# A spectral layer cut into 256 blocks at 160 frequencies in place of 128 blocks at 96

## The chip, the cores and the metric

The kernel runs on one core of a Trainium2 chip. The metric is device time in microseconds (us) of one execution, the median over the runs shown. The core has a matrix engine (TensorE, PE in the profile, with its weight loads as PEld), VectorE (DVE), ScalarE (ACT), GpSimd (POOL) and the sync engine (SP). SP and POOL also issue most of the DMAs. TensorE writes to PSUM, from where VectorE and ScalarE take the results.

## What is computed

Two layers on an input of 2 batches, 128 channels and 64x64 positions (L = 4096 tokens). Layer 0: a group norm, a four-head attention with rotary positions, a projection, a residual. Layer 1: a layer norm and a one-head attention over the tokens (`x x^T`, softmax, times `x`), a residual; then a layer norm and a spectral layer, with a residual. The spectral layer, cut to what matters:

```python
U_plus  = causal_conv(phi[:, k], u)             # for each of K = 16 filters, all lags 0..L-1
U_minus = sgn * causal_conv(phi[:, k], sgn * u) # sgn is +1 on even, -1 on odd positions
out  = einsum('btkd,k,kde->bte', U_plus,  sigma**0.25, M_phi_plus)
out += einsum('btkd,k,kde->bte', U_minus, sigma**0.25, M_phi_minus)
out += sum over i < 3 of (u shifted by i) @ M_u[i]
```

Four branches (the first L, L/2, L/4, L/8 tokens) are weighed by a hard choice, of which one remains. `U_plus` and `U_minus` differ in the sign of the odd lags alone, so the kernel holds filters of even and of odd lags (parity s = 0, 1), each mixed by its own matrix: the sum of the two M for even lags, the difference for odd ones.

## The kernel before

**Layer 0** (`layer0`, to 1040 us) goes through four units (batch, pair of heads). The loop over score tiles carries side work: a generator `beside` that is advanced a step at some of the places in a unit. In the last unit that is `beside_last` (L991): the norm of batch 0 for the next attention, the filters' transforms (`filters16`, L876), and the mixing matrices. What is left of it when the loop ends is run after it.

**Attention of layer 1** (`attend16`, L1301), batch 0 from 1040 to 1340 us and batch 1 to 1734 us, carries side work in the same way: for batch 0 `rest16` (L1080: masks, taps); for batch 1 `feed` of batch 0 (L1427) and then, by turns, the first loads of the spectral stage and `feed` of batch 1, what is left of which goes on in the spectral steps.

**How the convolution is cut.** The 4096 tokens are 128 blocks of 32 (NI). Over the blocks, the convolution is done in frequencies (96, NF16); within a block, directly. A step of `feed` takes four token tiles (128 blocks x 128 channels, f32), multiplies them by cosines and by sines (L1482, `pf`), the blocks in two pieces of 64, each on 64 of the array's 128 rows, and writes an upper and a lower f16 half of the result to memory (L1446, L1447, L1487, `rows16`). It also transposes tiles for the taps (`ar`, L1458), and ends with a last shifted transform (`pl`, L1523). The filters are transformed likewise to `tables16`.

**The spectral stage** (`spectral`, L1895) has 48 steps: batch, chunk of 16 frequencies (6), parity of the lags s, parity of the output ro. For each step:

- `fetch` (L1281) loads tokens two steps ahead (POOL, three buffers) and tables (SP, two sets of buffers, one per parity).
- `convolve16` (L1697) makes 8 tiles `pu` of PSUM in bursts of 3, 3 and 2. A tile takes 6 products of 64 rows and 512 columns: three terms (upper x upper, lower x upper, upper x lower) for each of two row groups g, which hold different frequencies. The 64 rows are real and imaginary part x 2 pieces x 16 positions. The 512 columns are 16 output positions x 2 x 16 filters. ScalarE takes the upper half out (L1719), VectorE the lower (L1720), into `xh` and `xl`.
- `mix16` (L1722) mixes the step before: 48 products of 128 x 128 matrices with 512 columns, each as two on 64 rows, which go to two banks of `acc`. It is put between the bursts in three parts. At the end `acc` is added to `oh` (L1738 to L1741).

All products of this stage are kept in the order written (`ordered`), so a burst, a third of the mixing and a step of side work take turns on TensorE. The tag `cv` (three buffers of two banks) holds the bursts' tiles and also those of the side work.

**Back to positions** (`back`, L1799) goes over 4 groups of four positions per (batch, ro): 8 transposes of `oh` (L1857), copies to SBUF (L1858), 8 f32 products with `gw` (L1871), a sum with the attention's part (L1875). Batch 0's runs beside batch 1's steps, (1, 0) beside the last step, (1, 1) after all of them, then the result is written out (L1893).

The loop of the steps:

```python
for _ in convolve16(u, tables_in[s], tokens_in[n % 3], *xs):
    next(late, None)      # a third of the mixing of the step before
    next(beside, None)    # a step of the side work
```

Of the kernel before, what the change touches and what calls it, by code (L numbers as in the profile page):

```python
# [22 lines left out]
P = 128  # L23
# [17 lines left out]
NF = P  # L41
# [6 lines left out]
NF16 = 96  # L48
NCH16 = 6
NS = NF16 // NCH16 // 2  # L50
LAG = 3
# [29 lines left out]
def conv_attn_hybrid(ctx: ExitStack, tc: tile.TileContext, io):  # L81
# [8 lines left out]
    gmat = const.tile([P, P], F32, name="gmat")  # L90
    nc.sync.dma_start(gmat, io["gmat"])
# [13 lines left out]
    nc.gpsimd.memset(spread[NF16:, :NK], 0.0)  # L105
# [31 lines left out]
    def group_norm(b, bank, p1, px):  # L137
# [4 lines left out]
        st = p1.tile([P, NQ, 6], F32, tag="gst", name=f"gst{b}")  # L142
        yield xn
# [30 lines left out]
        xb = xi.rearrange("p (j i) -> p i j", i=NI)  # L174
        for i in range(NQ):
            dst = xn[:, bass.ts(i, 512)].rearrange("p (i j) -> p i j", j=P)
            src = xb[:, 4 * i : 4 * i + 4, :]
            if b == 0 and i >= NQ // 2:
                nc.scalar.activation(dst, src, AF.Identity, bias=bi, scale=sc)
            else:  # L180
                nc.vector.tensor_scalar(dst, src, sc, bi, ALU.mult, ALU.add)
# [17 lines left out]
    def layer0(tok, px, last, side, beside_last):  # L199
# [3 lines left out]
        with ExitStack() as l0:  # L203
# [193 lines left out]
            norm = group_norm(0, bank, p1, px)  # L397
# [33 lines left out]
            for n, (b, pr) in enumerate(units):  # L431
                if n + 1 < len(units):
                    nxt = units[n + 1]
                    if nxt[1] == 0:
                        norm = group_norm(nxt[0], bank, p1, px)
                        xn = next(norm)
                        after = prepare(*nxt, xn)
                        beside = chain(beside, norm, after[3])
                    else:
                        after = prepare(*nxt, xn)  # L440
                        beside = chain(beside, after[3])
# [49 lines left out]
    def layer0_any(tok, px, last, side, beside_last):  # L491

        with ExitStack() as l0:
# [25 lines left out]
            def normed(b):  # L519
                steps = group_norm(b, bank, p1, px)  # L520
# [192 lines left out]
    tables16 = dram.tile([2, 2, NF16 // NS, 2, 2, NDI, NS, 2 * NK], F16, name="tables16")  # L713
    rows16 = [dram.tile([2, 2, DROWS, 2, NF16, C], F16, name=f"rows16_{b}") for b in range(B)]
# [3 lines left out]
    class LayerStats:  # L718


        def __init__(self, p, src, u):
            self.p, self.src, self.u, self.nm = p, src, u, None
            self.mv = p.tile([P, NT, 2], F32, tag="lmv", name=f"lmv{u}", bufs=1)
            self.rs = p.tile([P, NT], F32, tag="lrs", name=f"lrs{u}", bufs=1)

        def take(self, tiles):
            for n, t in enumerate(tiles):
                st = self.p.tile([P, 6], F32, tag="lst", name=f"lst{self.u}_{t}", bufs=2)
# [52 lines left out]
    def layers(st, layer0, in_halves):  # L781
# [70 lines left out]
        def branches16(spare):  # L852

            phi = spare.tile([P, 2, TROW], F32, tag="tab", name="phi16")
            aside.dma_start(phi, io["phi"])
# [9 lines left out]
            turned = new([P, 2, NF16], "turned")  # L865
            aside.dma_start(turned, io["fw16"])
            most = new([P, 8, NK], "phi_most")[:NF16]
# [8 lines left out]
        def filters16(spare):  # L876
            phi, turned, most = chosen[3]
            both = spare.tile([P, 2, L], F16, tag="ks", name="spectra")
            for s, q in ((s, q) for s in range(2) for q in range(2)):
                tb = both[:NF16, q, : 4 * 2 * TROW].rearrange("w (h i x) -> w h i x", h=2, i=2)  # L880
                tbr = tb.rearrange("w h i (o c k) -> w h i c o k", c=2, k=NK)
                lags = slice(0, P // (q + 1))
                for c in range(2):
                    ph = side[0](f"ph{s}_{q}_{c}")[:NF16, :TROW]
                    nc.tensor.matmul(ph, turned[lags, c, :], phi[lags, s, :], start=True, stop=True)
                    nc.vector.tensor_reduce(
                        most[:, 4 * q + 2 * s + c, :], ph.rearrange("w (o k) -> w k o", k=NK), AX.X, ALU.max,
                        apply_absolute_value=True,
                    )
                    ph = ph.rearrange("w (o k) -> w o k", k=NK)  # L890
                    nc.vector.tensor_scalar(tbr[:, 0, 0, c], ph, T_SCALE, None, ALU.mult)
                    nc.vector.scalar_tensor_tensor(
                        tbr[:, 1, 0, c], ph, T_SCALE, tbr[:, 0, 0, c], ALU.mult, ALU.subtract
                    )
                    yield
                    for h in range(2):
                        if c == 0:
                            nc.vector.tensor_copy(tbr[:, h, 1, 1], tbr[:, h, 0, 0])
                        else:
                            nc.vector.tensor_scalar(tbr[:, h, 1, 0], tbr[:, h, 0, 1], -1.0, None, ALU.mult)  # L900
                    yield
                for w in range(NS):
                    part = slice(NF16 // NS * w, NF16 // NS * (w + 1))
                    for h in range(2):
                        aside.dma_start(
                            tables16[s, h, :, :, q, :, w, :].rearrange("b i o x -> b i o x"),
                            tb[part, h].rearrange("b i (o x) -> b i o x", x=2 * NK),
                        )
                yield
            nc.vector.tensor_reduce(spread[:NF16, :NK], most.rearrange("p n k -> p k n"), AX.X, ALU.max)  # L910
# [80 lines left out]
        def beside_last(stage, spare=None):  # L991
            first_parts()
            stages = [stage(n) for n in range(1 if in_halves else 2)]
            stats = LayerStats(last, tok[0], "a0")
# [19 lines left out]
        gw = ffw.tile([P, 2, P], F32, name="gw")  # L1014

        def transform(p):

            fw = p.tile([P, 4, NF16 if in_halves else NF], F32, name="fw", bufs=1)
            aside.dma_start(fw, io["fw_96" if in_halves else "fw"])
# [3 lines left out]
        mask = ffw.tile([P, P], F32, name="mask")  # L1023
        own_mask = ffw.tile([P, 1], F32, name="own_mask")
# [55 lines left out]
        def rest16(p, steps):  # L1080
            wbr, top = chosen[:2]
            ends = p.tile([P, NBR, P], F32, name="ends")
            aside.dma_start(ends, io["ends"].partition_broadcast(P))
            mu_raw = p.tile([P, NBR, NU, C], F32, name="mu_raw")
            aside.dma_start(mu_raw, io["mu"].rearrange("i n d e -> d i n e"))
            ends_T = p.tile([P, NBR], F32, name="ends_T")
            aside.dma_start(ends_T, io["ends_T"])
            aside.dma_start(gw[:NF16], io["gw16"])
            yield from steps
            weighted_sum(mask, ends, top)  # L1090
            weighted_sum(own_mask, ends_T.unsqueeze(2), top)
            yield
            weighted_sum(mu, mu_raw, wbr)
            yield
            own = gw[:NF16]
            nc.vector.scalar_tensor_tensor(
                own, own, OUT_SCALE, mask[:NF16].unsqueeze(1).to_broadcast([NF16, 2, P]), ALU.mult, ALU.mult
            )
# [134 lines left out]
        STEPS = []  # L1233
        for b in range(B):
            for ch in range(NCH16):
                pairs = [(s, ro) for s in range(2) for ro in range(2)]
                if (b, ch) == (B - 1, NCH16 - 1):
                    pairs = [(0, 0), (1, 0), (1, 1), (0, 1)]
                STEPS += [(b, ro, ch, s) for s, ro in pairs]
# [3 lines left out]
        def fetch_tokens(n):  # L1243
            if n >= len(STEPS):
                return
            b, ro, ch, s = STEPS[n]
            row = FIRST[STREAM[ro, s]]
            for half, ut in enumerate(tokens_in[n % 3]):
                for g in range(2):
                    w0 = NS * (2 * ch + g)  # L1250
                    ordered(
                        nc.gpsimd.dma_start(  # L1252
                            ut[64 * g : 64 * g + 64],
                            rows16[b].rearrange("c p r h w d -> (c p) r h w d")[:, row : row + BP, half, w0 : w0 + NS, :],
                        )
                    )
                    yield

        def fetch_tables(ch, s, pieces=1):
            for half, tt in enumerate(tables_in[s]):  # L1260
                own = tables16[s, half, 2 * ch]
                size = BP // pieces
                for part in range(pieces):
                    ordered(
                        nc.sync.dma_start(
                            tt[:, part * size : part * size + size],
                            bass.AP(
                                tensor=own.tensor,
                                offset=own.offset + part * size * NS * 2 * NK,
                                ap=[[NDI * NS * 2 * NK, 8], [NS * 2 * NK, BP], [1, size * NS * 2 * NK]],  # L1270
# [4 lines left out]

        def first_fetch():
            yield from fetch_tables(0, 0, 4)
# [3 lines left out]
        def fetch(n):  # L1281
# [3 lines left out]
            if n == 0:  # L1285
                todo = (0, 1)
            else:
                b, ro, ch, s = STEPS[n - 1]
                rest = [step for step in STEPS[n:] if step[3] == s]
                if not rest or (rest[0][0], rest[0][2]) == (b, ch):  # L1290
                    return
                todo = (rest[0][2], s)
            for _ in fetch_tables(*todo):
                pass
# [132 lines left out]
        def feed(b, p, bank, fw, stats=None, gate=None):  # L1427
# [7 lines left out]
            if in_halves:  # L1435
                to = rows16[b].rearrange("c p r h w d -> w c p (r h) d")
            else:
# [11 lines left out]
            def taps(i, uT):  # L1449
# [12 lines left out]
                queue.dma_start(base[b][:, 4 * i : 4 * i + 4, :], oc)  # L1462
# [3 lines left out]
            for i in range(NQ):  # L1466
                while gate is not None and gate[0] <= i:
                    yield
                un = p.tile([P, 4, C], F32, tag="un", name=f"un{b}_{i}")
                if in_halves:  # L1470
                    stats.prepare(range(4 * i, 4 * i + 4), own_mask)
# [3 lines left out]
                for c in range(2):  # L1475
                    at = BP + 1 + 2 * i
# [640 lines left out]
```

## Time and profile before

| what | value |
|---|---|
| median of 3 runs | 2601.43 us (2595.63 to 2602.68) |
| profiled execution, its own time | 2609.66 us |
| its span, first to last instruction | 2607.8 us |
| granted TensorE clock, mean | 0.984 |
| busy: TensorE / weight loads | 2464.1 us (94%) / 1203.5 us (46%) |
| busy: VectorE / ScalarE / GpSimd | 1545.1 us / 1769.4 us / 488.6 us |
| moved by DMA | 227.10 MB |

How to read it: a line of a group gives the source line, the engine, the operation, what it writes and reads by the program's names, the shape, the count, then busy time and mean duration of one, then the idle time of the engine just before such instructions with what ended it. A TensorE form `64*128 64x512` is 64 rows of contraction, 128 columns of weights, 512 columns moved. Busy time is a union, so overlapping products count once. An f32 product leaves two records. A timeline line begins with the start and the length in us; a line of a windows table has the stretch, its length, then busy time and instruction count of each engine, granted clock, DMA share and GB/s.

### The profile page before, as it was taken

Reading aid. Unit: us, or ns where it says so; the run is one execution under the profiler, and the core shown is the slowest. Engines: PE = TensorE matmul, PEld = TensorE weight load, DVE = VectorE, ACT = ScalarE, POOL = GpSimd, SP = SyncE. Lnnn points to the kernel's source line nnn. Section 1 sums busy time; section 2 is a strip of 40 time slices with the busy share of each in tenths; the row PEclk is TensorE's granted clock in tenths of the full one; section 3 lists DMA queues with packets and bytes.
Section 4 is the critical chain, followed back from the end, with each engine's and each line's share of the span. In section 5 each row is a group of like instructions: output and inputs, shape, how many; then the busy total and the mean of one; then the engine's idle time right before and its main releaser. Section 6 shows DMA issues by size and latency. Waiting matters only on the chain.

```text
span 2607.8 us, 37833 instructions
## 1 busy us (share of the span) xinstructions
PE 2464.1 (94%) x14787; PEld 1203.5 (46%) x14787; DVE 1545.1 (59%) x2854; ACT 1769.4 (68%) x2055; POOL 488.6 (19%) x773
## 2 busy tenths in 40 slices
PE   5999999999999999999989989879999999999996
PEld 3555555555544445444433334334444444444444
DVE  6256366236617542978786565676666665666653
ACT  4999999999999988666665555545445444455541
POOL 2022022002304432100033321132211111111100
PEclk9999999999999999999998989999999999999999
DMA  5122122002205533767566667644444443544421
GB/s 153 37 63 60 54 69 53 7 15 75 63 5 80 101 57 28 139 120 133 101 113 127 120 114 136 103 96 111 107 104 106 105 101 84 136 104 98 98 49 59
DMA packets 329469, 227.10 MB, mean 87 GB/s; under 512 B 286816, under 2 KB 289536, under 8 KB 323392
## 3 DMA queue, kind: packets, MB, share of 16 engines
q1 hardware_dynamic: 277008, 141.92, 26.4%
q0 software_dynamic: 50832, 80.24, 14.9%
q8 instruction: 118, 1.93, 0.3%
q10 hardware_dynamic: 1440, 2.43, 0.3%
q14 instruction: 71, 0.58, 0.1%
HBM read 117.84 MB, written 26.64 MB: 55 GB/s over the span
## 4 chain that ended last, share of the span: by engine, by line
PE 39%; DVE 8%; DMA 7%; issue 3%; ACT 2%; SPq 1%; POOL 0%; DVEq 0%; ACTq 0%; POOLq 0%
PE m L1730 18%; PE cv L1708 9%; DMA eT<-pair 5%; PE od L1340 3%; DVE pair L1326 2%; PE y L1312 2%; PE oa L1340 2%; DVE both L1360 2%; PE bk L1871 1%; DMA tables_b<-tables 1%; PE pf L1482 1%; PE ar L1458 1%; ACT ey L1321 1%; PE vt L1857 1%; SPq L1331 1%
## 5 line engine op out<-in xcount | busy, mean ns | idle before, releaser
L470 ACT ACTIVATE e<-s 128x1536 f16<-128x1536 f32 (+1 forms) x704 | 938.0, 1426 | 49.1 <-PE s L214 44.5
L1719 ACT CAST x<-cv 128x1024 f16<-128x1024 f32 x384 | 365.9, 1018 | 307.0 <-PE cv L1708 304.7
L1720 DVE TENSOR_TENSOR x<-cv,x 128x1024 f16<-128x1024 f32 x384 | 448.2, 1219 | 202.1 <-ACT x L1719 201.9
L214 PE MATMUL s<-qs,ks 128*128 128x512 f16 x2048 | 560.3, 381 | 7.9 <-ACT e L470 3.8
L214 PE MATMUL acc<-e,v 128*97 128x512 f16 x2048 | 559.5, 380 | 8.4 <-DVE accs L418 5.9
L1730 PE MATMUL m<-x,mxr 64*128 64x512 f16 x3072 | 466.7, 376 | 0.0
L214 PEld LDWEIGHTS <-v 128*97 128x97 bf16 x2048 | 255.3, 125 | 222.7 <-issue 22.1
L1321 ACT ACTIVATE ey<-y,nshift 128x512 f32<-128x512 f32 x288 | 196.1, 686 | 194.3 <-PE y L1312 151.1
L214 PEld LDWEIGHTS <-ks 128*128 128x128 f16 x2048 | 200.8, 99 | 233.5 <-issue 51.0
L1730 PE MATMUL m<-x,mxl 64*128 64x512 f16 x1536 | 293.3, 377 | 0.0
L1730 PEld LDWEIGHTS <-mxr 64*128 64x128 f16 x3072 | 152.0, 94 | 179.9 <-issue 1.0
L1360 DVE SCALAR_TENSOR_TENSOR both<-eT 128x512 f16<-128x512 f16 x224 | 153.6, 686 | 115.6 <-DMA eT<-pair 113.2
L1312 PE MATMUL y<-bothT 128*128 128x512 f16 x864 | 206.2, 382 | 3.9 <-ACT ey L1321 3.0
L1252 POOL DMA_DIRECT2D tokens<-rows x192 | 117.6, 618 | 441.4 <-PE cv L1708 404.6
L1340 PE MATMUL od<-pair,hi 128*128 128x512 f16 x576 | 190.4, 392 | 9.9 <-DVE oT L1352 9.0
L1326 DVE TENSOR_TENSOR pair<-ey,pair 128x1024 f16<-128x1024 f32 x144 | 174.8, 1217 | 26.6 <-ACT pair L1325 26.3
L1708 PEld LDWEIGHTS <-tokens 64*128 64x128 f16 x2304 | 112.2, 94 | 154.1 <-issue 27.9
L418 DVE COPY accs<-acc 97x512 f32<-97x512 f32 x64 | 44.2, 691 | 213.6 <-PE acc L214 213.6
L1340 PEld LDWEIGHTS <-hi 128*128 128x128 f16 x1024 | 102.0, 100 | 134.2 <-issue 21.7
L1325 ACT CAST pair<-ey 128x1024 f16<-128x1024 f32 x144 | 150.6, 1046 | 5.9 <-DMA eT<-pair 3.6
L1708 PE MATMUL cv<-tables_b,tokens 64*128 64x512 f16 x1152 | 138.3, 379 | 8.3 <-DMA tables_b<-tables 5.7
L1340 PE MATMUL oa<-eT,hi 128*128 128x512 f16 x448 | 145.3, 385 | 0.0
(222 smaller groups left out, 2414.0 us busy)
## 6 DMA issues: line engine op xcount, KB each, us to landing
tokens<-rows POOLq DMA_DIRECT2D x192, 128.0 KB, 9.7
tables_b<-tables SPq DMA_DIRECT2D x24, 1024.0 KB
tables_e<-tables SPq DMA_DIRECT2D x22, 1024.0 KB
tab<-in_rot SPq DMA_DIRECT2D x32, 512.0 KB
rows<-uh POOLq DMA_DIRECT2D x128, 96.0 KB, 3.2
ks<-term POOLq DMA_DIRECT2D x112, 64.0 KB, 2.2
qs<-term POOLq DMA_DIRECT2D x112, 64.0 KB, 2.0
accs<-back SPq DMA_DIRECT2D x32, 128.0 KB
```

The costliest lines, as they stand in the source:

```text
L214: tc.keep_in_program_order(nc.tensor.matmul(*args, **kw))
L470: nc.scalar.activation(e[:, own, :], ps[:, own, :], AF.Exp, scale=SCORE_SCALE)
L1312: nc.tensor.matmul(ps[:, q, :], a[0][:, bass.ts(t, P)], c[0][:, bass.ts(i, 512)], start=(n == 0), stop=(n == 2),)
L1321: nc.scalar.activation(e[:, q, :], ps[:, q, :], AF.Exp, bias=nshift16, accum_out=den[:, t, i : i + 1])
L1325: nc.scalar.copy(pair[:, 0, own], e)
L1326: nc.vector.tensor_tensor(pair[:, 1, own], e, pair[:, 0, own], ALU.subtract)
L1340: nc.tensor.matmul(acc, a[0][:, own], pair(m, t), start=(start and t == 0 and n == 0), stop=(stop and t == 3 and n == 2),)
L1360: nc.vector.scalar_tensor_tensor(both, eT[:, 0, :, u, :], 1.0, eT[:, 1, :, u, :], ALU.mult, ALU.add, accum_out=den[:, 4 * i + u, j : j + 1],)
L1708: nc.tensor.matmul(pu[:, g, :], ut[own, at, :], tt[own, :, at, :], start=(n == 0), stop=(n == 2))
L1719: nc.scalar.copy(hi, pur)
L1720: nc.vector.tensor_tensor(lo, pur, hi, ALU.subtract)
L1730: nc.tensor.matmul(acc[:, g, :], m[lines], x[lines], start=(i == 0), stop=(i == len(products) - 1))
```

## The change

Blocks of 16 tokens, 256 of them (two halves of 128, NB), 160 frequencies (NF16), pieces of 64 blocks as before but four of them. The 64 rows of a convolution product are now 2 x 4 pieces x 8 positions, and its 512 columns are 2 lag parities x 8 output positions x 2 x 16 filters, so that one product serves both parities. There are 40 steps: batch, chunk of 16 frequencies (10), half of a chunk. A step has 8 tiles, one per (input parity `par`, frequency of the half). Each tile is taken out in two pieces per engine, by lag parity, to the output parity `par ^ s`. The mixing has 96 products (parity s now inside) of 256 columns: 2 output parities x 4 frequencies x 2 groups x 16.

```diff
-NF16 = 96
-NCH16 = 6
+NB = 2
+BQ = NI // 4
+NF16 = 160
+NCH16 = 10
 NS = NF16 // NCH16 // 2
+HS = NS // 2
+PARTS = (107, 107, 106)
+BACKS = (0, 53, 106)
+NBACK = 54
...
+        STEPS = [(b, ch, half) for b in range(B) for ch in range(NCH16) for half in range(2)]
...
+        def fetch_tables(n):
...
+            row = NS * 2 * NK
+            for half, tt in enumerate(tables_in[n % 2]):
+                for s in range(2):
+                    for g in range(2):
...
+                            nc.sync.dma_start(
+                                tt[64 * g : 64 * g + 64, BQ * s : BQ * s + BQ + s],
...
+        def convolve16(u, half, tables, ut, xs):
+            th, tl = tables
+            items = [(par, at) for par in range(2) for at in range(HS)]
             for burst in BURSTS:
                 pus = []
+                for par, at in (items[n] for n in burst):
+                    pu = pc.tile([P, 2, 512], F32, tag="cv", name=f"cv{u}_{par}_{at}", bufs=3)
+                    for n, (h, tt) in enumerate(((0, th), (1, th), (0, tl))):
...
+                                    ut[own, par, at, h, :],
+                                    filters_of(tt, own, par, HS * half + at),
...
                 yield
+                for par, at, pu in pus:
+                    pur = pu.rearrange("d g (s o k) -> d s k g o", s=2, k=NK)
+                    for s in range(2):
+                        hi, lo = (
+                            x[:, s].rearrange("d k (r w g o) -> d r w k g o", r=2, w=HS, g=2)[:, par ^ s, at] for x in xs
+                        )
+                        nc.scalar.copy(hi, pur[:, s])
+                        nc.vector.tensor_tensor(lo, pur[:, s], hi, ALU.subtract)
+                yield
+        def mix16(ch, half, xh, xl, acc, ohs):
+            products = [(m[:, k, s, :], xh[:, s, k, :]) for s in range(2) for k in range(NK) for m in (mxl, mxr)]
+            products += [(mxr[:, k, s, :], xl[:, s, k, :]) for s in range(2) for k in range(NK)]
...
+                if (i + 1) % (2 * NK) == 0:
                     yield
+            for ro, oh in enumerate(ohs):
+                part = acc[:, :, P * ro : P * ro + P].rearrange("e n (w q c) -> e n w q c", w=NS, c=2)
...
+                nc.scalar.copy(own, part[:, 0])
+                nc.vector.tensor_tensor(own, part[:, 1], own, ALU.add)
```

In the loop of the steps the evictions of a burst now come ahead of the side work. The other parts of the diff:

- `filters16`: eight groups (four shifts of 64 blocks, lines 128 and 32 of the frequencies) in place of four, each for cosine and sine; products over 256 lags are two accumulated ones where both halves hold something. The table's last dimension stays 32 f16 values (64 bytes) to a write.
- `feed`: three transforms (107, 107 and 106 lines of cosines and sines together) for four token tiles in place of two; the shifted last transform `pl` falls away; a half's edge is carried to the other half.
- `back16` in place of `back`: 4 groups of two positions per (batch, ro), with transposes of 108 columns for each of three parts (`BACKS`) and f32 products of 256 columns. For batch 1 the first two parts run beside the steps from the eighth chunk on, the third after the last step.

```diff
+            for q2 in range(BQ // 2):
...
+                for q, pt in enumerate(pair):
+                    for n, m in enumerate(chunks):
+                        ordered(nc.tensor.transpose(pt[:, n, :], ohr[:, BQ - 1 - 2 * q2 - q, own], ident))
+                for q, pt in enumerate(pair):
+                    (nc.scalar.copy if q else nc.vector.tensor_copy)(v[:, q, own, :], pt[:, own, :])
+                yield
+                for q in range(2):
+                    for n, m in enumerate(chunks):
...
+                                pt[:, q, :], v[:, q, n, :], gw[:, m, :], start=(n == 0), stop=(n == len(chunks) - 1)
...
+                nc.vector.tensor_tensor(dst, pt, hads[q2] if begin else dst, ALU.add)
```

- `gw` is scaled and masked at the start of batch 1's steps (`inverse_of`) in place of `rest16`; masks have 256 columns; the matrix `gmat` of the group norm is loaded anew for each batch; one buffer in place of two for the mixing matrices' loads; the statistics of the last unit move to other buffers; the tokens of a group norm are put in the order of the new halves.

## The prediction

> **What bounds the kernel now.** I read the stages first, then the groups of one stage, then the order of TensorE's work. By windows cut at the stage borders (0 to 1040 layer 0, to 1340 and to 1734 the attention of batch 0 and 1, to 2574 the spectral steps, then the tail):
>
> ```profile
> core 0: us, PE busy (x) PEld busy (x) DVE busy (x) ACT busy (x) POOL busy (x), PEclk, DMA share, GB/s
> 800.00:1040.00 240.00, 229.56 (x1029) 115.54 (x1027) 123.20 (x305) 221.26 (x169) 89.17 (x112) 0.99 0.47 67
> 1340.00:1734.00 394.00, 351.79 (x1428) 150.16 (x1426) 248.16 (x580) 219.45 (x460) 102.25 (x144) 0.94 0.64 117
> 1900.00:2142.00 242.00, 242.00 (x2243) 109.05 (x2240) 162.39 (x149) 123.05 (x133) 38.77 (x64) 1.00 0.47 102
> 2574.00:2608.00 34.00, 16.26 (x134) 14.79 (x132) 9.84 (x13) 2.91 (x5) 0.00 (x0) 0.89 0.17 65
> ```
>
> From 1900 to 2142 nothing but spectral steps runs: TensorE is busy all 242 us and issues 2243 products, 107.9 ns each. A step has 48 products of the convolution and 96 of the mixing, so it takes 144 x 107.9 = 15.54 us, and 48 steps take 746 us. VectorE has 162 of 242 us, ScalarE 123. So the spectral stage is bound by TensorE, and the question is what a step costs there. Groups of 1900 to 2100 by form:
>
> ```profile
> L1730 PE MATMUL m<-x,mxr 64*128 64x512 f16 x830 | 125.6, 376 | 0.0
> L1720 DVE TENSOR_TENSOR x<-cv,x 128x1024 f16<-128x1024 f32 x104 | 121.3, 1219 | 53.8 <-ACT x L1719 53.8
> L1719 ACT CAST x<-cv 128x1024 f16<-128x1024 f32 x104 | 99.0, 1018 | 86.5 <-PE cv L1708 86.1
> ```
>
> The mixing never waits (0.0); VectorE and ScalarE wait for TensorE, not it for them. TensorE's order of time, three answers:
>
> ```profile
> 1951.85 0.38 PE L1730 MATMUL m<-x,mxl 64*128 64x512 f16 x2
> 1952.06 0.38 PE L1730 MATMUL m<-x,mxr 64*128 64x512 f16 x2
> ...
> 1851.34 0.60 PE L1523 MATMUL pl<-un,fw 64*96 64x128 f32 x8
> ...
> 2592.52 3.74 PE L1871 MATMUL bk<-gw,whole 96*128 96x128 f32 x32
> ```
>
> Two products on 64 rows each run as a pair, one pair per 215.5 ns, though one record lasts 376 ns.
>
> **Main step: 48 steps become 40, and the mixing's products become half as wide.** The convolution keeps 48 products of 512 columns a step: 48 x 107.9 ns = 5.18 us. The mixing goes from 96 products of 512 columns to 192 of 256: the same columns, twice the products and weight loads. The trace has no f16 product of 256 columns, so this is bounded from both sides. Below: half of 215.5, 108 ns a pair. Above: nothing hidden, the width's 108 plus one 94 ns weight load (mean of the mixing's loads), 202. Two rows lie near. An f32 record takes twice as long per column: six `ar` records of 512 columns take 2.74 us, one alone 0.592, so (2.74 - 0.592) / 5 = 430 ns. An f32 record of 128 columns thus streams as long as an f16 one of 256. The `bk` row (one row group): (3.74 - 0.275) / 31 = 112 ns per load and product. The `pl` row has the very form of the new mixing, pairs on 64 rows, each with its own loads: 8 in 0.60 us, one alone 0.269, so (0.60 - 0.269) / 3 = 110 ns a pair, with f32 loads that last longer (159 ns) than the f16 ones (94).
>
> A rule of the Trainium skill speaks against it: "TensorE: Matmul & The Clock Gate", section Back-to-back issue gap, has streams of weight load and product at some 81 ns a product for 128 columns, whatever the formula for an isolated one gives. If a load and its product cost 81 ns here too, a pair takes 162. The `pl` row says 55 a product, but for 8 products that could have been queued; 192 in a row are not shown. I take 110 and keep 162 as a rival.
>
> Step after: 5.18 + 96 x 0.110 = 15.74 us; 40 steps 630 us. **746 - 630 = 116 us gained.** Each ns of the pair costs 96 x 40 = 3.84 us.
>
> **The engines beside it.** The 8 evictions of 1024 elements by each engine become 16 of 512. Rows of this size: ScalarE 586 ns (`oh<-m`), VectorE 690 (`oh<-m,oh`). ScalarE: 16 x 0.586 + 2 x 0.27 for the accumulator = 9.9 us of 15.74; VectorE 16 x 0.69 + 2 x 0.3 = 11.6. Both stay below TensorE. Within a burst, six VectorE pieces end about 5.6 us after its start, and the third buffer is wanted at 6.7. So these cost nothing while TensorE is the slower; uncovered, VectorE sets the step (a rival). The writes are runs of 32 bytes; L891 writes such runs (96x496) in 653 ns, no slower. Token loads stay four of 128 KB a step. Tables become 2.2 MB each two steps after 2.1 MB, again asked for two steps ahead: hidden. The one stall for them (5.7 us, the first `tables_b`) I keep.
>
> **Feed (to frequencies).** Two transforms for every four token tiles become three, so the 128 `pf` records become 192. Four records (one transform) take 0.86 us (1.02 less the 0.16 that one record's end takes). In the spectral steps the last three sets of token tiles stay over as before: 3 more transforms, +3 us, less the `pl` work and stall (1.5), plus about 2 of waits for the shared buffers: +3. In the attention of batch 1: 13 more, 11 us; the waits there grow by half, less the `pl` stall:
>
> ```profile
> PE pf L1482 <- DVE uh L1447: 12.4, 10, 2.9
> PE pl L1523 <- DVE oc L1461: 5.6, 1, 5.6
> PE uT L1504 <- DVE uh L1447: 5.0, 3, 3.3
> ```
>
> (17.4 + 4.8 for `un`) / 2 = 11, less 6 for `pl` and less some 4 as gaps overlap: with the products **+12 us**. POOL issues 192 row writes for 128 at 0.68 us, behind token loads on the same queue; it has 102 of 394 us busy, so this is hidden.
>
> **Filters in layer 0.** In 800 to 1040 TensorE is busy 230 and ScalarE 221 of 240 us: no room on either. The filters' f32 products go from 8 (two records each, 0.83 us) to 24 of 0.86: +14 us TensorE. VectorE gets 96 operations for 40, +25 us; it has 117 us idle there, but each holds the one bank that the output projection uses: +3. The side work needs 100 turns where the loop offers 96, and now used 80: the last four run after it, with 3 us of VectorE exposed at most. 64-byte table writes grow from 47,616 to 81,920 and are needed only some 500 us later. **+17 us.** Masks twice as wide in attention 0: +1.
>
> **Back.** Before, a group of four positions takes 8 transposes (1.1 us) and 16 records of `bk` (1.95), and waits 0.78 us between the transposes: 3.8 us, 10 groups before the last mixing ends, 38 us. After, a group of two takes 6 transposes (0.85) and 12 records of 256 columns (0.216 each, 2.6): 8 groups for batch 0, 28 us; for batch 1 two thirds beside the steps, 18 us; some 2 us of waits, the transposes now standing before both copies. 48 less 38: **+10**. Tail: before 24.8 us from the last mixing product to the last sum. After, 8 groups with a third each; every one waits in a ring, copy 0.27, products 1.02, sum 0.95 (L1875 takes 1.03), signals 0.2: 2.45 us, with the accumulator's eviction 21.5. **-3.** The output's 9.6 us stay.
>
> **Sum.** -116 + 3 + 12 + 17 + 1 + 10 - 3 = -76; first ramp of the steps (VectorE's 16 x 0.69 after 8 x 1.22) +1: -75. The profiled execution took 2609.7 us (span 2607.8), so 2534.7; the median of the runs stands 8.2 below it: 2601.4 - 75 = **2526 us**.
>
> **Rivals.**
> - *Loads or issue set the mixing's pace* (other side). For: four instructions per 110 ns is twice the present rate, and 480 a step for 288; the rule above. Against: `pl` at that very rate. At 162 ns, + 52 x 3.84 = 200: 2726. It decides from 110 + 75 / 3.84 = 129.5 ns on; at 135 the time is 2622. Chance 0.16.
> - *VectorE becomes the bound.* For: strided sums (L1875) take 1.03 us at 512 elements where others take 0.69. At that price 16 x 1.03 + 0.8 = 17.3 us a step, less what of the back and feed work on TensorE now lies beneath it: about +35, 2561. Against: the 32-byte runs of L891. Chance 0.12.
> - *Side work costs double* (filters and feed, 29 us more, by in-order waits in both): 2555. For: TensorE's 42 idle us in attention 1 lie around such waits. Chance 0.12.
> - *Side work is absorbed* in the idle 10 us of layer 0's end and 42 of attention 1: 2500. Chance 0.10.
>
> **How the numbers follow.** The forecast's chance is 0.50; its own range is 2505 to 2550 (pair 108 to 114, side terms by half). A difference under 0.3% (7.8 us) can't be told from none. Faster: 0.50 + 0.10 + 0.12 + 0.09 of VectorE's = 0.81; same 0.03, from VectorE's far end; slower 0.16. The range reaches from the absorbed case to where pairs stand near 135 ns: 2490 to 2622; past it remain 0.12 above and 0.05 below.
>
> **What would show it.** Right: in mid-stage, pairs of `m` start every 110 ns, TensorE busy throughout, steps of 15.7 us, the spectral stage some 105 us shorter, layer 0 some 17 and attention 1 some 12 longer. Wrong: pairs further apart with no releaser named (issue); `cv` waiting for DVE `x`; `po` or `pf` waiting for VectorE by tens of us.

## The result, and the profile after

The changed kernel takes 3088.45 us (3081.52 to 3095.21), 1.187 times the time before (95% interval 1.183 to 1.191). The forecast was 2526 us, with a range of 2490 to 2622. The profiled execution has a span of 3093.4 us and a mean granted clock of 0.899 (0.984 before).

Cut at the same events as before (first score of each batch's attention, first product of the convolution, last of the mixing), in us, with the experiment that matters most beside it (e1: the same change with pieces of 112, 112 and 96 lines):

| stage | before | after | after - before | e1 | e1 - before |
|---|---|---|---|---|---|
| layer 0 | 1041.1 | 1065.6 | +24 | 1064.3 | +23 |
| attention, batch 0 | 276.2 | 304.0 | +28 | 303.4 | +27 |
| attention, batch 1 | 417.1 | 896.4 | +479 | 452.7 | +36 |
| spectral, to the last mixing | 839.1 | 792.8 | -46 | 747.8 | -91 |
| tail | 34.3 | 34.7 | 0 | 35.3 | +1 |

The loss lies in one stage, the attention of batch 1. The windows of that stage and of the middle of the spectral stage, of the changed kernel (columns as before: the stretch, its length, busy time and count by engine, clock, DMA share, GB/s):

```profile
1370.00:2266.00 896.00, 442.92 (x1568) 180.32 (x1567) 300.42 (x681) 248.28 (x515) 450.51 (x193) 0.73 0.72 64
2800.00:3055.00 255.00, 254.21 (x3692) 188.68 (x3688) 168.98 (x278) 137.37 (x268) 35.20 (x53) 1.00 0.33 86
```

In the spectral steps TensorE works 254 of 255 us. In the attention of batch 1 it works 443 of 896; POOL is busy 451 us there, where it had 102 of 394. The waits of 1370 to 2266 us (who waits, for whom, sum, times, longest):

```profile
ACT uh L1461 <- DMA rows<-uh: 345.7, 21, 30.8
...
DVE uh L1462 <- ACT uh L1461: 275.4, 21, 33.0
...
PE uT L1530 <- DVE uh L1462: 211.8, 12, 28.6
...
PE pf L1504 <- DVE uh L1462: 129.1, 17, 21.4
```

Read from the top, this is a chain. ScalarE may write `uh`, of which there are two buffers, only when the row writes out of it have landed. VectorE stands behind ScalarE, and TensorE behind VectorE for the next transform or transpose; what the attention has behind these in the engines' order waits with them. ScalarE's group of these evictions over the whole kernel, before and after:

```profile
L1446 ACT ACTIVATE uh<-pf 96x512 f16<-96x512 f32 x64 | 37.1, 592 | 56.4 <-PE pf L1482 50.2 <-DVE uh L1447 5.2 <-DMA rows<-uh 0.6
...
L1461 ACT ACTIVATE uh<-pf 107x512 f16<-107x512 f32 (+1 forms) x96 | 55.6, 596 | 501.3 <-DMA rows<-uh 388.0
```

The wait for the row writes was 0.6 us and is 388, in 24 pieces, each of which ends 0.1 to 0.4 us after the last row write of the transform two before has landed. The row writes themselves, as groups of POOL and as DMA issues with the median from issue to landing, before:

```profile
L1487 POOL DMA_DIRECT2D rows<-uh x128 | 87.1, 686 | 120.9 <-DVE uh L1447 98.8 <-DMA tokens<-rows 12.4 <-DVE both L1360 4.4
...
rows<-uh POOLq DMA_DIRECT2D x128, 96.0 KB, 3.2
```

and after:

```profile
L1509 POOL DMA_DIRECT2D rows<-uh x192 | 517.8, 2700 | 232.5 <-DVE uh L1462 138.5 <-issue 91.4 <-DMA rows<-uh 1.4
...
rows<-uh POOLq DMA_DIRECT2D x128, 107.0 KB, 15.0
...
rows<-uh POOLq DMA_DIRECT2D x64, 106.0 KB, 20.2
```

A write of 107 or 106 KB in place of 96 KB costs POOL four times as long to issue (2700 ns mean for 686) and lands some five to six times as late (15.0 and 20.2 us for 3.2). The forecast had 192 of them at 0.68 us.

What the forecast was about did happen. TensorE's order of time in the spectral steps of the changed kernel (start, length, products of the run):

```profile
2884.59 2.11 PE L1751 MATMUL cv<-tables_b,tokens 64*128 64x512 f16 x18
2886.54 0.27 PE L1779 MATMUL m<-x,mxl 64*128 64x256 f16 x2
2886.65 0.27 PE L1779 MATMUL m<-x,mxr 64*128 64x256 f16 x2
...
2889.92 0.27 PE L1779 MATMUL m<-x,mxr 64*128 64x256 f16 x2
2890.03 2.11 PE L1751 MATMUL cv<-tables_b,tokens 64*128 64x512 f16 x18
```

From 2886.54 to 2889.92 are 31 pairs, 109.0 ns each, and a burst with its third of the mixing takes 5.44 us (2890.03 - 2884.59), as 18 x 107.9 ns + 32 x 110 ns = 5.46 us would have it.

### The profile page after: what moved, and what is told of

The parts are those of the page before. It is cut to its first block, busy times and chain, and to the rows that moved or that the text cites. A ratio compares the mean times of both kernels' runs of the same rounds, so it can differ in the third digit from the quotient of the medians.

```text
span 3093.4 us, 44325 instructions
## 1 busy us (share of the span) xinstructions
PE 2458.0 (79%) x17459; PEld 1364.1 (44%) x17459; DVE 1543.5 (50%) x3219; ACT 1777.5 (57%) x2399; POOL 926.4 (30%) x800
## 3 DMA queue, kind: packets, MB, share of 16 engines
q0 software_dynamic: 134560, 90.46, 19.0%
q10 hardware_dynamic: 1440, 2.43, 0.2%
## 5 line engine op out<-in xcount | busy, mean ns | idle before, releaser
L1509 POOL DMA_DIRECT2D rows<-uh x192 | 517.8, 2700 | 232.5 <-DVE uh L1462 138.5
L1767 ACT CAST x<-cv 128x512 f16<-128x512 f32 x640 | 355.2, 589 | 271.4 <-DVE x L1768 172.7
L1768 DVE TENSOR_TENSOR x<-cv,x 128x512 f16<-128x512 f32 x640 | 415.7, 686 | 174.3 <-ACT x L1767 169.7
L1779 PE MATMUL m<-x,mxr 64*128 64x256 f16 x5120 | 433.4, 270 | 0.0
L1461 ACT ACTIVATE uh<-pf 107x512 f16<-107x512 f32 (+1 forms) x96 | 55.6, 596 | 501.3 <-DMA rows<-uh 388.0
L1779 PE MATMUL m<-x,mxl 64*128 64x256 f16 x2560 | 287.2, 271 | 1.3 <-DVE oh L1789 1.3
L1779 PEld LDWEIGHTS <-mxr 64*128 64x128 f16 x5120 | 253.5, 95 | 46.5 <-issue 1.2
L1462 DVE SCALAR_TENSOR_TENSOR uh<-pf,uh 107x512 f16<-107x512 f32 (+1 forms) x96 | 64.2, 685 | 327.5 <-ACT uh L1461 327.4
L1504 PE MATMUL pf<-un,fw 64*107 64x512 f32 (+1 forms) x192 | 86.3, 739 | 150.7 <-DVE uh L1462 130.4
L1530 PE MATMUL uT<-ident,un 128*128 128x128 f32 x64 | 16.4, 406 | 218.0 <-DVE uh L1462 218.0
```

Source lines behind the costliest of these rows:

```text
L1509: queue.dma_start(rows16[b][r, 2 * part + q, at : at + 2, lines].rearrange("t w h d -> w t (h d)"), uh[:, q, 2 * r : 2 * r + 2].rearrange( ...
L1767: nc.scalar.copy(hi, pur[:, s])
L1768: nc.vector.tensor_tensor(lo, pur[:, s], hi, ALU.subtract)
L1779: nc.tensor.matmul(acc[:, g, :], m[lines], x[lines], start=(i == 0), stop=(i == len(products) - 1))
```

## The experiments

Three questions: what makes the row writes slow, what took the main step's gain once they are mended, and whether a version exists that keeps it.

My theory after the result: the count of lines of a row write is what hurts, 107 being prime and 106 = 2 x 53. The Trainium skill, "DMA: Bandwidth & Descriptors", section "Why a DMA increments its semaphore by 16 and not by 1", says that a transfer runs on as many of the 16 engines as the largest number up to 16 that divides the slowest dimension of both its sides: 16 for 96 lines, 1 for 107, 2 for 106. It names an exception for POOL's queue that could have spared these writes, so the rule is put to the test. Rivals: more writes on POOL's queue, or a busier memory, whatever the count.

**e1 and e2: the same change with other pieces.** The three transforms have 320 lines together however they are cut.

```diff
-PARTS = (107, 107, 106)
+PARTS = (112, 112, 96)      # e2: (128, 128, 64)
```

> The changed kernel, the three transforms of feed cut into 112, 112 and 96 lines in place of 107, 107 and 106; nothing else. Uneven-lines theory (a row write whose line count has no divisor near 16 is issued slowly and lands late): POOL's row writes fall from 2.7 us each to about 0.7 and land in 3 to 5 us instead of 15, the attention of batch 1 goes from about 890 back to some 405 us, the kernel to 2540 to 2580 us. Rival, count theory (half again as many writes and transforms through two buffers): nothing of this, the kernel stays above 2950 us.

> The changed kernel with parts of 128, 128 and 64 lines. Uneven-lines theory: within 15 us of the run with 112, 112 and 96. If the number of lines in one write counts, and not its divisors, it is slower than that run by more than 15 us. Count theory: above 2950 us.

Measured: e1 2608.78 us, ratio 1.0025 (1.0014 to 1.0035); e2 2605.9 us, 1.002 (1.001 to 1.0029). The number of writes is the same 192. The row writes of e1:

```profile
L1509 POOL DMA_DIRECT2D rows<-uh x192 | 125.2, 658 | 161.4 <-DVE uh L1462 156.9
...
rows<-uh POOLq DMA_DIRECT2D x128, 112.0 KB, 2.5
...
rows<-uh POOLq DMA_DIRECT2D x64, 96.0 KB, 2.9
```

One constant takes away 480 us: larger writes (112 KB) land after 2.5 us, and the mean issue takes 658 ns. The number of writes and their bytes are not the cause. ScalarE's wait for the writes falls from 388 to 21.1 us. Still, e1 only comes level with the kernel before; 2540 to 2580 us were expected, and the attention of batch 1 at 405 us, where it takes 452.7. The later experiments look for this rest.

**e3 and e4: the kernel before, each row write split in two.** In e3 at an odd place, in e4 in halves.

```diff
-queue.dma_start(to[:, c, q, 2 * own : 2 * own + 4, :], uh[:, q, 2 * r : 2 * r + 2]...)
+for w in (slice(0, 53), slice(53, NF16)):      # e4: (slice(0, 48), slice(48, NF16))
+    queue.dma_start(to[w, c, q, 2 * own : 2 * own + 4, :], uh[w, q, 2 * r : 2 * r + 2]...)
```

> The kernel before, each row write of 96 lines issued as two, of 53 and 43 lines; nothing else of the change. Uneven-lines theory: 256 writes at about 2.5 to 3 us each on POOL and landing late: slower by 250 to 600 us, all of it in the attention of batch 1 and the first spectral steps. Count theory: the same time as the run with two of 48 lines.

> The kernel before, each row write of 96 lines issued as two of 48. Uneven-lines theory: 256 writes at about 0.65 us each: at most 25 us slower. Count theory: slower by 100 us or more, as the one with 53 and 43.

Measured: e3 3349.24 us, ratio 1.287 (1.284 to 1.290); e4 2604.24 us, 1.0015 (1.0001 to 1.0029). In e3:

```profile
L1488 POOL DMA_DIRECT2D rows<-uh x256 | 523.1, 2046 | 540.0 <-issue 488.3
...
L1446 ACT ACTIVATE uh<-pf 96x512 f16<-96x512 f32 x64 | 36.5, 591 | 483.0 <-DMA rows<-uh 335.7
...
rows<-uh POOLq DMA_DIRECT2D x128, 53.0 KB, 20.6
rows<-uh POOLq DMA_DIRECT2D x128, 43.0 KB, 19.1
```

and in e4:

```profile
L1488 POOL DMA_DIRECT2D rows<-uh x256 | 148.0, 586 | 108.0 <-DVE uh L1447 72.2
...
rows<-uh POOLq DMA_DIRECT2D x256, 48.0 KB, 2.3
```

The fault can be put into the kernel before, by nothing but the place of a cut: the same bytes in the same 256 writes differ by 745 us (3349.24 - 2604.24). That is the theory's sharpest test (e3 was expected 250 to 600 us slower; it is 748). The writes of 43 lines land after 19 us with less than half the bytes of the 96 KB write that lands in 3.2.

**e5: 108, 108 and 104 lines.** None of these is a multiple of 16; the largest divisors up to 16 are 12, 12 and 13.

> The changed kernel with parts of 108, 108 and 104 lines. If a write goes over as many DMA engines as the largest number up to 16 that divides its lines (12 and 13 here), it is nearly as quick as with 112, 112 and 96: at most 40 us slower than that run. If only multiples of 16 are quick and every other count takes the slow way of 107, it stays above 2950 us.

Measured: 2614.02 us, ratio 1.0059 (1.0041 to 1.0077). POOL takes 758 ns a write, landing 2.7 us (108 lines) and 4.2 (104). So it needs no 16: 12 or 13 come within 0.3 to 0.4% of it. Only counts whose largest divisor up to 16 is 1 or 2 were slow here; what lies between was not run.

**e10: the 107-line writes issued by SP.** Is it POOL's issue that costs, or the transfer?

```diff
-                                queue.dma_start(
+                                nc.sync.dma_start(
```

> The changed kernel with its 107, 107 and 106 lines, the row writes issued by the sync engine's hardware queue in place of POOL's. Issue theory (POOL makes the descriptors of an uneven write one by one, 3.1 us each, and that alone is the loss): the writes land in 3 us or so, the kernel at 2590 to 2660 us. Spread theory (an uneven write goes over one or two DMA engines whoever issues it): they land in 7 us and more, ScalarE waits for its two buffers, and the transposes of the attention stand behind the writes on the same queue: 2700 to 3100 us.

Measured: 3146.1 us, ratio 1.210 (1.208 to 1.212). ScalarE's group of the row evictions, with what ended its idle time:

```profile
L1461 ACT ACTIVATE uh<-pf 107x512 f16<-107x512 f32 (+1 forms) x96 | 55.9, 597 | 513.2 <-DMA rows<-uh 377.9 <-PE pf L1504 127.0 <-DVE uh L1462 6.8
```

With POOL out of it ScalarE waits 378 us for the same writes (388 in the changed kernel). So the loss goes with the writes and not with POOL. SP is slow to issue them too (4.9 us median, 0.2 at the least), and the attention's transposes stand in the same queue, so this run alone does not part issue from transfer. In the changed kernel the two can be told apart: a 107-line write takes 3.1 us to issue and lands 15 us after its issue began, so most of the time lies behind the issue.

The sizes of the packets in the traces show how the writes were spread. On SP's queue in e10 the rows are 40,960 packets of 512 bytes, just their data, and 256 packets of 4 bytes come with them: one for each of the 128 writes of 107 lines, two for each of the 64 of 106. On POOL's queue the changed kernel has, against e1, more packets of 24 bytes (1920 = 128 x 15), of 8 bytes (896 = 64 x 14) and of 32 bytes (61,568 = 128 x 15 x 26 + 64 x 14 x 13). That fits one reading: a 107-line write sends its data over one DMA engine, as 26 packets of 4096 bytes and one of 3072, and a 106-line write over two, as 13 of 4096 and one of 1024 on each; every engine without data gets as many small packets. These counts of engines, 1 and 2, are those of the rule tested here, on both queues. e10 has no small packets and loses as much, so they are not needed for the loss.

**e6: a seventh turn of side work in the last part of layer 0** (on e1). e1 leaves some 50 us over the kernel before in layer 0 and the attention of batch 0. TensorE stands there right after the first scores of batch 0, in e1:

```profile
PE y L1329 <- ACT ey L1338: 23.2, 2, 21.3
```

ScalarE has not yet taken these scores out. The profile names the loads of the masks as what ScalarE waits for, but the landings tell otherwise: the last table write of the filters is issued after layer 0's loop and lands at 1087.8 us, ScalarE starts at 1088.4, and the masks' loads land after that (`ends` 1091.6, `ends_T` 1094.3). So it is the last table writes that hold it. Before, the last of them had landed at 1006.8 us, 34 us ahead of the first scores.

```diff
-BESIDE_LAST = (0, 1, 3, 5, 6, 9)
+BESIDE_LAST = (0, 1, 3, 5, 6, 9, 10)
```

> Parts of 112, 112 and 96, and the side work of layer 0's last unit is also advanced at the tenth score tile (7 turns a row of tiles in place of 6, 112 in all for the 100 needed). Late-writes theory (the last filter group is emitted after the loop, its eight table writes hold the start of attention 0 by some 21 us): the first wait of TensorE in attention 0 for ScalarE is gone, the kernel 15 to 27 us faster than with 112 lines alone, about 2585. Rival, loads theory (that wait is for the masks' and taps' loads, which come after layer 0 in any case): within 6 us of that run.

Measured: 2606.87 us, ratio 1.002 (1.0008 to 1.0031), no gain where 15 to 27 us were expected. The 21-us wait is gone (3.0 us in three), the attention of batch 0 is 22 us shorter (280.9), and layer 0 is 25 us longer (1089.0). TensorE's output projection `po` now waits for VectorE's `ao`:

```profile
PE po L224 <- DVE ao L392: 20.8, 2, 11.4
```

The stall moved.

**e7 and e8: the scaling of the inverse table `turn`** (on e1). At about 1991 us, POOL issues the load of `turn`; VectorE stands at its scaling until it has landed, and TensorE waits for the convolution's evictions behind it. Waits of e1 from 1960 to 2030 us (the load is named here by another DMA of the same queue):

```profile
DVE turn L1967 <- DMA had<-base: 13.9, 1, 13.9
...
PE cv L1751 <- DVE x L1768: 12.4, 2, 12.0
```

e7 makes the scaling a step of the side work, three turns after the load; e8 keeps it in that place in VectorE's order as well:

```diff
-            nc.vector.scalar_tensor_tensor(turn, turn, OUT_SCALE, own, ALU.mult, ALU.mult)
-            return turn
+            def scaled():
+                ordered(nc.vector.scalar_tensor_tensor(turn, turn, OUT_SCALE, own, ALU.mult, ALU.mult))  # e7: without ordered
+                yield
+            return turn, scaled()
...
-                    beside = chain([None] * 3, *parts, guard(one_bank))
+                    beside = chain([None] * 3, scaled, *parts, guard(one_bank))
```

> Parts of 112, 112 and 96, and the inverse transform's matrices are scaled three turns after their load is issued, not right behind it. Blocked-queue theory (VectorE stands 13.9 us before the scaling, and the convolution's evictions stand behind it): TensorE's one wait of 12.0 us for VectorE at the start of batch 1's steps is gone, 8 to 13 us faster than with 112 lines alone. Rival: the wait comes from draining the side work at that place, and stays: no difference.

> The kernel with pieces of 112, 112 and 96 lines, and with the scaling of the inverse transform's table kept at its place in VectorE's order, three turns of the side work after its load is issued (moving the line in the program alone changed nothing: VectorE still stood 11.9 us for the load). Theory that VectorE's 13.9-us stand at the table's load is what costs TensorE the 12.0-us wait for the convolution's eviction at the change of batch: 2597 to 2600 us, 9 to 12 us under the 2608.8 of the same kernel without it, and the long wait of cv for x gone. Rival, that the stand is only moved to the first product of the way back, or was covered by other work: 2606 to 2611 us.

Measured: e7 2607.52 us, ratio 1.0023 (1.0003 to 1.0042), with VectorE still standing 11.9 us at 2005 us: its place in the program did not move it, and it stays some 200 us ahead of the first product that reads `turn` (2211 us in e1). e8 2592.46 us, ratio 0.9966 (0.9954 to 0.9977), somewhat more than the 9 to 12 us expected: the long waits of `turn` and of `cv` are gone, and the spectral stage is 15 us shorter than in e1 (732.8).

**e13: table writes in runs of 128 bytes** (on e1). The table writes of the filters land after 9.8 us in e1, 5.5 before; layer 0's last round trips through memory (4 KB each) and the first loads of the attention run among them. The two halves of a number are put side by side in memory, and a buffer holds four frequencies with both halves in place of eight with one. Bytes and products stay.

```diff
-    tables16 = dram.tile([2 * NCH16, 2, 2, 2, 4, NDQ, NS, 2 * NK], F16, name="tables16")
+    tables16 = dram.tile([2, 2 * NCH16, 2, 2, 4, NDQ, HS, 2, 2 * NK], F16, name="tables16")
...
-                            tables16[first : first + groups, :, :, :, q, :, w, :].rearrange(
-                                "b s h i o x -> b (s h i) o x"
+                            tables16[w // HS, first : first + groups, :, :, q, :, w % HS].rearrange(
+                                "b s i o h x -> b (s i) o (h x)"
```

> The kernel with pieces of 112, 112 and 96 lines, and with the filters' tables laid out in DRAM so that each piece of a table write is 128 bytes for 64 (the two halves of a number side by side): 40,960 pieces for 81,920, where the kernel before has 47,616; products, evictions and fetched bytes as they are. Theory that the pieces of the table writes hold up layer 0's small round trips and the start of attention 0: landing of the table writes back from 9.8 us to about 5, the 21-us wait at attention 0's start mostly gone, layer 0 and attention 0 together 25 to 40 us shorter than the 50 us that they have over the kernel before, so 2570 to 2585 us. Rival, that layer 0 is longer for the filters' products and evictions themselves (14 us of TensorE more): not more than 8 us gained, 2600 to 2610 us.

Measured: 2581.94 us, ratio 0.9912 (0.9898 to 0.9926). The table writes of e1:

```profile
tables<-spectra POOLq DMA_DIRECT2D x32, 128.0 KB, 9.8
```

and of e13:

```profile
tables<-spectra POOLq DMA_DIRECT2D x32, 128.0 KB, 6.2
```

TensorE's wait at the start of the attention, in e13:

```profile
PE y L1329 <- ACT ey L1338: 13.8, 2, 11.9
```

Layer 0 and the attention of batch 0 are 22 us shorter than in e1 (1345.4 for 1367.7 together), a little less than the 25 to 40 expected: the wait went from 21.3 to 11.9 us, not to nothing. The last table write lands at 1065.1 us and ScalarE starts at 1065.7, 15 us after the first scores (24 in e1); VectorE's operations on the filters last as long as they did or 0.1 us less. So the small runs account for 22 of the 50 us that these two stages had lost.

**e14 and e15: both together, and with the seventh turn.**

> Both of the last two edits on the pieces of 112, 112 and 96 lines: 128-byte pieces in the table writes, and the scaling of the inverse table at its place. If both losses are what the theory says, they add, for they lie in different stages: 2558 to 2575 us, faster than the kernel before. If each is covered by a wait behind it: 2600 to 2608 us.

> The last kernel with a seventh turn of the side work in each step of layer 0's last part, so that the filters end before attention 0 begins. With the long pieces of 64 bytes this moved the stall from attention 0 to layer 0 and gained nothing. If the stall is the writes' traffic, then with half of the pieces there is nothing left to move: within 6 us of the kernel without the seventh turn. If it is the filters' work on TensorE and VectorE, a seventh turn gains up to 15 us in attention 0 and loses up to 25 in layer 0.

Measured: e14 2570.92 us, ratio 0.9876 (0.9861 to 0.9891); e15 2568.19 us, 0.9875 (0.9859 to 0.9891). The two edits nearly add, as edits in different stages should (27 us for e13 and 16 for e8 against e1's median, 38 together), and e14 is 1.2% faster than the kernel before. In e15 the attention of batch 0 is 15 us shorter than in e14 and layer 0 12 us longer, with no net gain. With the writes eased, this is the pattern that e15's expectation gave to the filters' own work: it has to be done in one of the two stages. That is read from the stages; no run took this work away alone, and the time by itself (within 6 us of e14) fits both theories of that expectation.

## Why the prediction was wrong

**The step that failed** is in the part on the feed: "POOL issues 192 row writes for 128 at 0.68 us ... so this is hidden". The duration came from a row for 96 lines, and was carried to 107 lines as if only the count of writes mattered. It measured 2.70 us to issue and 15 to 20 us to land, and the second is what costs: `uh` has two buffers, so the whole feed goes at the writes' pace. e1 undoes just this and is 480 us shorter by the medians, 490 by the profiled spans. Of the 490, 444 lie in the attention of batch 1 and 45 in the spectral steps (896.4 - 452.7, 792.8 - 747.8), where the rest of the feed runs. None of my rivals was this one. The pieces (107, 107 and 106) stood in the change, and what such counts do to a DMA could have been looked up; I weighed a rule on TensorE's issue and not the one on DMAs.

Mended, e14's stages can be held against the sum:

| term | forecast | measured (e14 - before) |
|---|---|---|
| spectral stage: main step, feed there, back, ramp | -102 | -105 |
| feed in the attention of batch 1 | +12 | +37 |
| filters in layer 0, masks | +18 | +9 in layer 0, +18 in the attention of batch 0 |
| tail | -3 | +3 |
| sum | -75 | -37 (span 2570.6 for 2607.8) |

**Main step: right.** 110 ns a pair were forecast from eight `pl` products; 109.0 were measured over 31 pairs in a row, in step after step. The rival of loads and issue (162 ns) fell, and so did VectorE as the bound: TensorE works 254 of 255 us. The spectral stage came out at some 105 us shorter as said, once e8 had taken off a term that was not in the sum at all: the load and scaling of `turn` (12 to 15 us), which I read in the change and gave no price.

**Feed in the attention of batch 1: mis-sized, +37 for +12.** The groups of TensorE's transforms in that stage, before:

```profile
L1482 PE MATMUL pf<-un,fw 64*96 64x512 f32 x104 | 43.6, 666 | 17.5 <-DVE uh L1447 12.4 <-ACT un L758 4.8
```

and in e14:

```profile
L1504 PE MATMUL pf<-un,fw 64*112 64x512 f32 (+1 forms) x156 | 69.2, 725 | 30.2 <-DVE uh L1462 25.4 <-ACT un L769 2.5 <-DVE tok L1401 1.8
```

52 records more cost 25.6 us of busy time, 0.49 each, where I had 0.86 / 4 = 0.215 from the record's length within one run of four. The group's own row before has 43.6 / 104 = 0.42 a record: a mean over the stage, in which the runs are broken by waits and the clock is at 0.94. The waits before them grew by 12.7 us where the forecast had 11 in all, less 10 for `pl` and for overlap. Busy time and waits come to 38 us; `pl` (1.9 + 5.6) is off again, and smaller waits grew (`uT` from 5.0 to 10.1 us, `ar` from 0 to 2.6), which leads to about the 37 measured.

**Filters: two terms mis-sized.** The table writes were put at nothing, since their result is needed late. Their traffic is not late: it slowed the transfers beside it, and halving the runs' number was worth 22 us over the two stages. And "3 us of VectorE exposed at most" for the turns left over was measured as TensorE's wait of 21.3 us at the start of the attention, of which the lighter writes left 11.9. What the turns left over exposed was not VectorE's work but these writes: ScalarE takes out the first scores only when the last of them has landed (1087.8 and 1088.4 us in e1), so their result is needed at once and not "some 500 us later". Why the program has ScalarE wait for them was not looked into.

**Tail:** I had 2.45 us for each turn of the ring, from durations at full clock. The first turns of the changed kernel kept to it; the last did not; two of each, by their products:

```profile
3065.12 1.13 PE L1880 MATMUL bk<-turn,v 108*128 108x256 f32 x4 [1.07 <-DVE v L1874]
...
3067.55 1.13 PE L1880 MATMUL bk<-turn,v 108*128 108x256 f32 x4 [1.07 <-DVE v L1874]
...
3076.39 2.07 PE L1880 MATMUL bk<-turn,v 108*128 108x256 f32 x4 [0.87 <-DVE v L1874]
...
3079.76 2.08 PE L1880 MATMUL bk<-turn,v 108*128 108x256 f32 x4 [0.87 <-DVE v L1874]
```

A turn takes 2.43 us at first and 3.37 at the end, where four products last 2.07 us for 1.13. The granted clock over that window is 0.67 in the changed kernel, 0.59 in e14 and was 0.89 before, and the gain of 3 us became none (after) or a loss of 3 (e14).

## What to carry to other kernels

Before a tile's count of lines is changed, look at its divisors: of the counts tried here, those with no divisor from 3 to 16 (43, 53, 106, 107) made a DMA write land in 15 to 21 us, while 48, 64, 96, 104, 108, 112 and 128 lines landed in 2.2 to 4.2. Price a DMA by its whole shape, and ask who waits for its landing and with how many buffers, not only what its issue costs. For side work take the mean of the group over its stage, not the best run of the timeline, and price every new load with the operation that waits for it.

## What was not expected of the hardware

The writes of 107 and 106 lines also came with more packets: POOL's queue has 134,560 in the changed kernel for 71,072 in e1, 331 more for each of the 192 writes, at nearly the same bytes (90.46 MB for 88.44). These are the small packets counted under e10. The exception that the skill's section names for POOL's queue, which would spread such counts over most of the engines all the same, did not show: the packets fit data on one and two engines, and the writes were as harmful from POOL's queue as from SP's. The few engines do not explain the whole landing time. Where nothing disturbs them, packets of 4096 bytes start 0.16 to 0.18 us apart, so an estimate for 27 in a row is somewhat under 5 us; with 3.1 us of issue that is about half of 15. What makes up the rest stays open, and so does why 106 lines land later than 107.

In the attention of batch 1 of the changed kernel the granted clock fell to 0.73 with TensorE busy half of the time (443 of 896 us). In e1 the same stage has 0.93, with TensorE busy 398 of 453 us for the same products. So of the 444 us between the two some 45 are busy time that came with the lower clock, and the stall cost more than its own length.

Sustained pairs on 64 rows with a weight load each ran at 54.5 ns a product of 256 columns, two thirds of the 81 ns that the rule weighed in the prediction would have given.
